# Fetching the values of even batches in two parts, and one chain of finishing steps for all twenty heads

## The chip, the cores and the metric

The kernel runs on one core of one Trainium2 chip. The metric is the device time of one execution in microseconds. The median of three runs of the kernel before is 429.22 us (427.91 to 430.65). The core has five engines that run side by side and wait for each other by semaphores: PE (TensorE), DVE (VectorE), ACT (ScalarE), POOL (GpSimd) and SP (SyncE, which here only issues transfers).

## The reference

Attention of 112 queries over 371 text tokens and 4 prompt tokens, for 8 batches and 20 heads of 16 channels, all in float32. The text probabilities are used a second time: the weighted mean of the context (512 wide) is normalised, and its inner products with the normalised prompts are added to the prompt scores.

```python
text_ehs = encoder_hidden_states[:, :-NUM_TOKENS]
ip_ehs = encoder_hidden_states[:, -NUM_TOKENS:]
...
probs_t = jax.nn.softmax(scores_t, axis=-1)
text_out = jnp.einsum('bhst,bhtd->bhsd', probs_t, v_t)
...
attn_scores = jnp.einsum('bhsd,bhnd->bhsn', q, k_ip) * attn_scale
qsem = jnp.einsum('bhst,bte->bhse', probs_t, text_ehs)
qsem = _l2norm(qsem)
ip_n = _l2norm(ip_ehs)
sem = jnp.einsum('bhse,bne->bhsn', qsem, ip_n)
fused = attn_scores + SEM_SCALE * sem
probs_ip = jax.nn.softmax(fused, axis=-1)
probs_ip = probs_ip * spatial_mask[None, None, :, None]
ip_out = jnp.einsum('bhsn,bhnd->bhsd', probs_ip, v_ip)
...
out = text_out + IP_SCALE * ip_out
out = out @ W_out + b_out
out = out + residual
```

## The kernel before

The twenty heads are worked on in five groups of four (`groups`), one step per batch and group; `b` is the batch, `g` the group, `a` the head within it. The kernel never forms the weighted context. It uses the matrix of inner products of the context rows with each other (the Gram matrix, `gram`, in the tile `ug`), so that the squared norm for a head is the probabilities times that matrix times the probabilities. The matrix is symmetric, so only its upper part is kept, with half weight on the diagonal blocks.

For each head the right operand of the products is a row of blocks in the tile `u`: the inner products of a block of 32 tokens with the tokens from there on, then the four prompts, a column of ones, and the 16 value channels of the head. One product round `j` (there are twelve, `BLK`) multiplies 32 transposed probability rows with such a block for the four heads of the group, each head in its own row band of the array and its own bank (`product`, L711 to L724). The bank then holds, for one head, the probabilities times the matrix (371 columns, read by `reduced` or `shared` to make the squared norm `ss`), and 21 further columns (the prompt products, the sum of probabilities, the values' sum), copied by ACT to `pvs` (`value_sums`).

How `u` is filled for a batch:

- The inner products: `gram_to_groups(b, (q,))` (L484) issues four transfers from `ug` to `u` for quarter `q` of the blocks, one for each row band. All four quarters are needed.
- The values: `values` makes them on PE in three chunks of 128 tokens (`vext`); `values_to_dram` (L561) writes them to DRAM (`vd`), `values_to_groups` (L581) fetches them back in the order of the row bands (`vr`), and before each group `placed` (L629) copies the group's 16 channels, chunk by chunk, from `vr` into `u` on POOL. Chunk `c` serves the product rounds 4c to 4c+3.

The probabilities take a similar way: `scores` on PE, `probabilities` (maximum on DVE, exponential on ACT, then a transfer `xg<-p` from SP), and `transposed` on DVE turns `xg` into `xgT`. Scores are made two groups ahead (`LEAD`).

The order of instructions on every engine is the order of the program text. Two steps are interleaved by `pair`, what has to be made for the next batches stands in `behind` (L1219), and pieces of work are generators that are advanced by `f`, `k`, `v`, `gr`, `q` and `run`. `turn` lists from which of three pools (`qd` four banks, `sc` two, `mm` two) the next banks of the array's output come. In an odd batch, `moved` (L1204) transfers the quarters 0, 1 and 3 behind the groups 0, 1 and 2, `behind` does quarter 2 at group 1, and the last chunk of values goes to DRAM at group 3 with the fetch of all values behind it (L1311 to L1320):

```python
            values_to_dram(nb, nc.sync, 2)
            tr(0)
            k(nb)
            f(b - 1, 2)
            tr(1)
            values_to_groups(nb)
```

`finish` turns `ss` and `pvs` of a batch into its output: a root and a reciprocal for the norm, a softmax over four prompts per head, the weighted prompt values, the division by the sum of probabilities, the output projection and the residual. ACT needs one table for the root and another for the exponential, loaded by `preload_act_table`.

The last batch (7) has no successor to interleave with, and its order is written out at the end (L1344 to L1427). There some heads' squared norms are made by ACT and POOL instead of DVE (`shared`: ACT copies the bank, POOL multiplies, ACT adds up). Batch 6 is finished within batch 7: `finish(b - 1, bd=...)` begins at group 1, takes its root at group 2, and its last projections stand behind the last product. Batch 7 itself is finished in two chains: `finish(b, (0, FULL * HC), ...)` for the first sixteen heads, begun before the last group's products, and `last_heads` for the last four; `projected_prompts` multiplies the last four heads' prompt values with the output matrix beforehand. The third key chunk of batch 7 is made by `last_keys` (L522) in two halves with two scores between.

Of the kernel before, what the change touches and what calls it, by code (L numbers as in the profile page):

```python
# [20 lines left out]
def kernel(  # L21
# [500 lines left out]
    def last_keys(b, ps):  # L522

        s = st[b]
        for e in range(NE):
            if e == NE // 2:
                yield
            nc.tensor.matmul(
                ps[:, :TT],
                wk_sb[:, e, FULL * P :],  # L530
                s["ctxT"][:, e, :TT],
                start=(e == 0),
                stop=(e == NE - 1),
            )
        nc.scalar.copy(s["kT"][:, FULL, :TT], ps[:, :TT])
        yield
# [44 lines left out]
    def values_to_groups(b):  # L581
        s = st[b]
        w = NG * D
        for a in range(GROUP):
            nc.sync.dma_start(
                s["vr"][a * RG : (a + 1) * RG].rearrange("p j g d -> p j (g d)"),
                s["vd"][:, a * w : (a + 1) * w].rearrange("(j i) x -> i j x", i=RG),
            )
# [86 lines left out]
    def probabilities(b, g, a):  # L675
# [13 lines left out]
        if (b, g, a) == (B - 1, NG - 1, 1):  # L689
            s["third"] = rows, p  # L690
            return
        nc.sync.dma_start(rows, p)
        if "third" in s:
            nc.scalar.dma_start(*s.pop("third"))
# [47 lines left out]
    def value_sums(b, g, a0=0):  # L742
        s = st[b]
        for h, ps in list(zip(groups[g], s["qd", g]))[a0:]:
            nc.scalar.copy(s["pvs"][:, h, :], ps[:S, TT:UW])  # L745

    def shared(b, g, n):
# [3 lines left out]
        if b == B - 1:  # L751
            t = work.tile([P, NE, TP], F32, tag="ctxT", name=f"shared_{b}_{g}")
            prods = [t[:S, a, :TT] for a, _ in some]
        else:

            t = work.tile([S, NIP, H, D], F32, tag="wv", name=f"shared_{b}_{g}", bufs=1)
            t = t.rearrange("p n h d -> p (n h d)")
            prods = [t[:, a * TP : a * TP + TT] for a, _ in some]
        p = s["p", g]
        for a, (h, ps) in some:  # L760
            if b == B - 1:
                nc.scalar.copy(s["pvs"][:, h, :], ps[:S, TT:UW])  # L762
# [32 lines left out]
    def finish(b, heads=(0, H), bd=None):  # L795
# [3 lines left out]
        h0, h1 = heads  # L799
        n = h1 - h0  # L800
        part = slice(h0, h1)

        def sm(name):
            return small.tile([S, H], F32, tag=name, name=f"{name}_{b}_{h0}", bufs=1)[:, :n]

        def sm4(name):
            return small.tile([S, H, NIP], F32, tag=name, name=f"{name}_{b}_{h0}", bufs=1)[:, :n]

        def over_ip(t):
            return t.unsqueeze(2).to_broadcast([S, n, NIP])  # L810

        pvs = s["pvs"][:, part]
# [8 lines left out]
        nc.vector.tensor_tensor(rn, s["ss"][:, part], z2, ALU.max)  # L821
        zr = sm("zr")
        attn = attn_ring[b % 2]
        ah = attn[:, :C].rearrange("p (h d) -> p h d", d=D)[:, part]

        def divided():
            eng.tensor_tensor(
                ah, pvs[:, :, NIP + 1 :], zr.unsqueeze(2).to_broadcast([S, n, D]), ALU.mult
# [17 lines left out]
        nc.vector.scalar_tensor_tensor(fu, fu, SEM_SCALE, s["ipl"][:, part], ALU.mult, ALU.add)  # L846
# [17 lines left out]
        i0, i1 = h0 * D // P, -(-h1 * D // P)  # L864
        if bd is not None:
            ps = bank(f"ps_wT_{b}")
            nc.tensor.transpose(
                ps[: n * NIP, :S], w.rearrange("s h n -> s (h n)"), ident[:S, :S]
            )
            wT = work.tile([P, NE, TP], F32, tag="ctxT", name=f"wT_{b}")[:, 0, :S]  # L870
            nc.scalar.copy(wT[: n * NIP], ps[: n * NIP, :S])
            yield

            ps = bank(f"ps_a_{b}_{h0}")
            for i in range(i0, i1):
                o = ps[:, i * S : (i + 1) * S]
                nc.tensor.matmul(  # L877
                    o, attn[:, i * P : (i + 1) * P], ident[:S, :S], start=True, stop=False
                )
                nc.tensor.matmul(  # L880
                    o,
                    bd[: n * NIP, i * P : (i + 1) * P],
                    wT[: n * NIP],
                    start=False,
                    stop=True,
                )
            yield

            aT = work.tile([P, NC, S], F32, tag="aT", name=f"aT_{b}_{h0}")
            nc.scalar.copy(  # L890
                aT[:, i0:i1], ps[:, i0 * S : i1 * S].rearrange("p (i s) -> p i s", s=S)
            )
            yield

            s["o"] = bank(f"ps_o_{b}", spare=True)
            for i in range(i0, i1):
                nc.tensor.matmul(  # L897
                    s["o"][:S, :C], aT[:, i, :], wo_sb[:, i, :], start=(i == 0), stop=(i == NC - 1)
                )
            if h1 < H:  # L900
                yield
                return
            yield
        else:
            yield from prompt_sums_and_projection(b, s, eng, part, n, h0, i0, i1, w, attn, ah)

        ob = work.tile([S, C], F32, tag="ob", name=f"ob_{b}", bufs=1)
        nc.vector.tensor_tensor(ob, s["o"][:S, :C], s["xb"], ALU.add)
# [6 lines left out]
    def prompt_sums_and_projection(b, s, eng, part, n, h0, i0, i1, w, attn, ah):  # L915
        wv = work.tile([S, NIP, H, D], F32, tag="wv", name=f"wv_{b}_{h0}", bufs=1)[:, :, :n]
        eng.tensor_tensor(
            wv,
            s["vip"][:, :, part],
            w.rearrange("p h n -> p n h").unsqueeze(3).to_broadcast([S, NIP, n, D]),  # L920
            ALU.mult,
        )
        eng.tensor_tensor(wv[:, :2], wv[:, :2], wv[:, 2:], ALU.add)
        eng.tensor_tensor(ah, ah, wv[:, 0], ALU.add)
# [546 lines left out]
```

## Time and profile before

| | |
|---|---|
| median of three runs | 429.22 us (427.91 to 430.65) |
| the profiled execution's own time | 432.04 us |
| its span, first to last instruction | 430.3 us |
| mean granted clock of PE | 0.995 |
| busy PE, DVE, ACT, POOL | 417.9, 330.5, 189.5, 111.6 us |
| transfers | 64.28 MB in 58063 packets, 18880 of them under 512 B |
| fetch of values, `vr<-vd` | 32 transfers of 120 KB |
| inner products, `u<-ug` | 128 transfers of 99 KB |
| probabilities, `xg<-p` | 159 transfers of 162.3 KB from SP, one from ACT |

Times in the profile are microseconds from the start of the span unless marked ns. A row of a timeline gives the start, the duration, the engine, the line and operation, the output and inputs, the count of merged instructions, and in brackets the engine's idle time before it and what ended it. SPq rows are the issuing of transfers, not their course. A row of a window table gives the window and its length, the busy time of PE, its weight loads, DVE, ACT and POOL with instruction counts, then the granted clock of PE, the busy share of the transfer engines and GB/s. Each float32 matmul shows as two instructions.

### The profile page before, as it was taken

What the parts mean: (1) busy time and instruction counts of PE and PEld (TensorE: products, weight loads), DVE (VectorE), ACT (ScalarE), POOL (GpSimd) and SP (SyncE); (2) the same over time, 40 slices, a digit from 0 to 9 for tenths busy, and PEclk for the clock granted to TensorE, in tenths of its full rate; (3) what the DMA queues carried; (4) which work ended last, traced back from release to release, by engine and by line L of the source; (5) the groups of instructions that cost most, each with busy time, mean ns of one, the idle gap of its engine ahead of it and who ended that gap; (6) DMA issues with size and microseconds to landing.
All of it is one profiled execution on the core that took longest, in us unless ns stands there. A gap on an engine that the chain in (4) does not pass through costs nothing. (4 is left out here: it accounts for less than half of the span.)

```text
span 430.3 us, 14013 instructions
## 1 busy us (share of the span) xinstructions
PE 417.9 (97%) x5515; PEld 325.6 (76%) x5515; DVE 330.5 (77%) x688; ACT 189.5 (44%) x646; POOL 111.6 (26%) x272
## 2 busy tenths in 40 slices
PE   8999999999999999999998999999997999999986
PEld 8766677797768887777677796879675887776783
DVE  4045877898888977877987887887988597778884
ACT  3253342336335642334542652515542364336793
POOL 4303110021332260031150351021060126026440
PEclk9999999999999999999999999999999899999999
DMA  7678967887553756767554746657655236663300
GB/s 246 166 195 240 199 167 184 177 185 171 134 144 104 173 146 158 175 138 177 133 157 122 174 123 159 164 135 170 169 138 144 79 102 168 162 161 107 97 2 28
DMA packets 58063, 64.28 MB, mean 149 GB/s; under 512 B 18880, under 2 KB 52024, under 8 KB 57998
## 3 DMA queue, kind: packets, MB, share of 16 engines
q1 hardware_dynamic: 57432, 62.67, 57.7%
q8 instruction: 44, 0.72, 0.7%
q10 hardware_dynamic: 566, 0.72, 0.5%
q14 instruction: 21, 0.17, 0.1%
HBM read 18.67 MB, written 5.32 MB: 56 GB/s over the span
## 5 line engine op out<-in xcount | busy, mean ns | idle before, releaser
L718 PE MATMUL ps_qd<-u,xgT 32*112 32x232 f32 (+11 forms) x3840 | 218.0, 354 | 4.9 <-POOL u L633 4.9
L718 PEld LDWEIGHTS ps_qd<-u,xgT 32*112 32x112 f32 x3840 | 186.2, 173 | 36.3 <-issue 8.4
L706 DVE STREAM_TRANSPOSE xgT<-xg 128x768 f32<-128x768 f32 (+1 forms) x63 | 122.2, 1970 | 3.9 <-DMA xg<-p 3.8
L683 ACT ACTIVATE p<-ps_s,nmx 112x371 f32<-112x371 f32 x160 | 85.6, 584 | 54.5 <-DVE nmx L679 42.6
L778 DVE CUSTOM_DVE_ANT_0 junk<-ps_qd,p 112x371 f32<-112x371 f32 x148 | 80.2, 542 | 34.8 <-ACT pvs L745 11.4
L679 DVE TENSOR_REDUCE nmx<-ps_s 112x1 f32<-112x371 f32 x160 | 77.2, 535 | 28.4 <-PE ps_s L666 27.0
L633 POOL COPY u<-vr 128x64 f32<-128x64 f32 x120 | 26.5, 236 | 200.6 <-PE ps_qd L718 113.1
L546 PE MATMUL ps_v<-wv_sb,ctxT 128*128 128x384 f32 (+1 forms) x192 | 63.8, 479 | 0.3 <-ACT kT L519 0.3
L666 PE MATMUL ps_s<-kT,qm 32*112 32x375 f32 (+1 forms) x320 | 61.0, 486 | 0.7 <-ACT shared L763 0.7
L546 PEld LDWEIGHTS ps_v<-wv_sb,ctxT 128*128 128x128 f32 x192 | 35.3, 190 | 21.2 <-ACT kT L519 1.2
L745 ACT COPY pvs<-ps_qd 112x21 f32<-112x21 f32 x150 | 21.3, 199 | 65.6 <-DVE ss L778 64.3
L512 PE MATMUL ps_k<-ctxT,wk_sb 128*128 128x371 f32 x136 | 45.8, 481 | 0.0
L512 PEld LDWEIGHTS ps_k<-ctxT,wk_sb 128*128 128x128 f32 x136 | 24.6, 190 | 13.4 <-ACT ctxT L424 0.5
L474 PE MATMUL ps_g<-ctxT 128*32 128x119 f32 (+11 forms) x672 | 33.3, 344 | 0.6 <-POOL ctxT L390 0.6
L666 PEld LDWEIGHTS ps_s<-kT,qm 32*112 32x112 f32 x320 | 28.4, 171 | 5.3 <-ACT shared L763 1.3
L474 PEld LDWEIGHTS ps_g<-ctxT 128*32 128x32 f32 x672 | 25.9, 110 | 8.1 <-issue 4.1
L553 ACT COPY vext<-ps_v 128x384 f32<-128x384 f32 (+1 forms) x24 | 11.2, 465 | 37.1 <-PE ps_v L546 37.0
L685 ACT COPY ipl<-ps_s 112x4 f32<-112x4 f32 x140 | 24.1, 172 | 0.0
L519 ACT COPY kT<-ps_k 128x371 f32<-128x371 f32 x17 | 8.0, 469 | 30.7 <-PE ps_k L512 30.7
L460 ACT ACTIVATE ug<-ps_g 128x375 f32<-128x375 f32 (+2 forms) x24 | 9.0, 377 | 27.9 <-PE ps_g L474 22.4
L353 DVE TENSOR_SCALAR qm<-ps_q,emask 128x224 f32<-128x224 f32 (+1 forms) x25 | 8.9, 396 | 15.4 <-PE ps_q L344 15.4
L402 DVE STREAM_TRANSPOSE ctxT<-ct 128x512 f32<-128x512 f32 x18 | 19.1, 1067 | 0.0
(161 smaller groups left out, 318.7 us busy)
## 6 DMA issues: line engine op xcount, KB each, us to landing
xg<-p SPq DMA_DIRECT2D x159, 162.3 KB
u<-ug SPq DMA_DIRECT2D x128, 99.0 KB
ct<-in_ctx_dram SPq DMA_DIRECT2D x24, 176.0 KB
vr<-vd SPq DMA_DIRECT2D x32, 120.0 KB
vip<-vipd SPq DMA_DIRECT2D x6, 560.0 KB
vd<-vext SPq DMA_DIRECT2D x14, 160.0 KB
vd<-vext SPq DMA_DIRECT2D x28, 40.0 KB
out_dram<-ob SPq DMA_DIRECT2D x8, 140.0 KB
```

Source lines behind the costliest of these rows:

```text
L474: nc.tensor.matmul(ps[p * RG : (p + 1) * RG, s0 : T - t0], ctxT[:, e, t0 + q * RG : t0 + (q + 1) * RG], ctxT[:, e, t0 + s0 : T], start=(e ...
L512: nc.tensor.matmul(ps[:, :TT], wk_sb[:, e, i * P : (i + 1) * P], s["ctxT"][:, e, :TT], start=(e == 0), stop=(e == NE - 1),)
L546: nc.tensor.matmul(ps[:, :w], ctxT[:, e, c * P : (c + 1) * P], wv_sb[:, e, :w], start=(e == 0), stop=(e == NE - 1),)
L633: nc.gpsimd.tensor_copy(region(b, c)[:, :, UV - c * P :], s["vr"][:, c * QN : (c + 1) * QN, g, :])
L666: nc.tensor.matmul(ps[:S, :w], qm[a * RG : (a + 1) * RG, i, r, j * S : (j + 1) * S], s["kT"][a * RG : (a + 1) * RG, i, :w], start=True, st ...
L679: nc.vector.tensor_reduce(nmx, ps[:S, :TT], AX.X, ALU.max, negate=True)
L683: nc.scalar.activation(p, ps[:S, :TT], AF.Exp, bias=nmx)
L685: nc.scalar.copy(s["ipl"][:, groups[g][a], :], ps[:S, TT:T])
L706: nc.vector.transpose(xT[:, j : j + n].rearrange("p j (k q) -> p q j k", q=QN), xg[:, :, j * RG : (j + n) * RG].rearrange("p q (j k) -> p ...
L718: nc.tensor.matmul(banks[a][:S, j * RG : UW], xT[a * RG : (a + 1) * RG, j, :S], region(b, c)[a * RG : (a + 1) * RG, p, q * RG :], start=(j ...
L745: nc.scalar.copy(s["pvs"][:, h, :], ps[:S, TT:UW])
L778: nc.vector.tensor_tensor_reduce(out=junk, in0=ps[:S, :TT], in1=s["p", g][:, a, :], scale=1.0, scalar=0.0, op0=ALU.mult, op1=ALU.add, accu ...
```

## The change

First, in the odd batches 1, 3 and 5 (which prepare the batches 2, 4 and 6), `values_to_groups` takes a range of chunks. Behind group 2 it fetches chunks 0 and 1, where the last quarter of inner products was transferred. At group 3 that quarter is transferred behind the last chunk's way to DRAM, and the fetch of chunk 2 follows it.

Second, the last batch. The finishing of batch 6 starts behind group 4 of batch 6 (root and table loads included) and its weights are made at group 1 of batch 7; all four heads of batch 6's last group go to `reduced` on DVE. `last_keys` runs in one piece in an `sc` bank. The scores of the last group come at rounds 1 and 2 of group 2, heads 0 and 1 first, and two of the four transfers of their probabilities are issued by ACT. The first chunk of `placed` for the last group is copied ahead of the products that POOL makes for group 2's heads. `finish` loses its range of heads, `last_heads` and `projected_prompts` go, and `ending` finishes all twenty heads of batch 7 in one chain behind the last product: it transposes the attention of sixteen heads, multiplies the prompt values of all heads with the output matrix (`ps_bw`), takes the root for all heads at once, and sums attention and prompts in one bank (`ps_o`).

```diff
-    def values_to_groups(b):
+    def values_to_groups(b, c0=0, c1=NT):
         s = st[b]
         w = NG * D
         for a in range(GROUP):
             nc.sync.dma_start(
-                s["vr"][a * RG : (a + 1) * RG].rearrange("p j g d -> p j (g d)"),
-                s["vd"][:, a * w : (a + 1) * w].rearrange("(j i) x -> i j x", i=RG),
+                s["vr"][a * RG : (a + 1) * RG, c0 * QN : c1 * QN].rearrange(
+                    "p j g d -> p j (g d)"
+                ),
+                s["vd"][c0 * P : c1 * P, a * w : (a + 1) * w].rearrange("(j i) x -> i j x", i=RG),
             )
...
             if g == 2:
-                gram_to_groups(nb, (3,))
+                values_to_groups(nb, 0, 2)
...
             tr(1)
-            values_to_groups(nb)
+            gram_to_groups(nb, (3,))
+            values_to_groups(nb, 2)
...
-        if (b, g, a) == (B - 1, NG - 1, 1):
-            s["third"] = rows, p
-            return
-        nc.sync.dma_start(rows, p)
-        if "third" in s:
-            nc.scalar.dma_start(*s.pop("third"))
+        eng = nc.scalar if (b, g) == (B - 1, NG - 1) and a % 2 else nc.sync
+        eng.dma_start(rows, p)
...
+        elif b % 2 == 0:
+            turn[:] = ["qd"] * 4 + ["mm"]
+            q(nb, 2)
+            f(b - 1)
+            k(nb)
+            nc.scalar.preload_act_table(AF.Sqrt)
+            tr(0)
+            f(b - 1, 2)
+            run(("f", b), lambda: finish(b, bd=bd[:, 0]), 2)
...
+    places = {
+        0: {0: (2, 3), 1: (0, 1)},
+        1: {0: (1, 2)},
+        2: {1: (0, 1), 2: (2, 3)},
+    }
     for g in range(NG):
         if g == 1:
-            keys3 = last_keys(b, ps_qd.tile([P, 512], F32, tag="qd", name=f"ps_k_{b}_{FULL}"))
-            next(keys3)
+            run(("f", b - 2), None)
+            last_keys(b, ps_sc.tile([P, 512], F32, tag="sc", name=f"ps_k_{b}_{FULL}"))
+            run(before, None, 2)
             coming(g, (3, 0))
-            next(keys3)
-            run(before, lambda: finish(b - 1, bd=bd[:, 0]))
+            run(before, None)
             own_channels(bd)
             with_bias(b)
...
+            if g == 3 and j == 3:
+                placed(b, g + 1, (0,))
+                next(sums)
+                transposed(b, g + 1)
+                drain(sums)
+            elif g < 3 and j == 2:
+                drain(sums)
+                transposed(b, g + 1)
...
+    drain(sums)
+    last = ending(b, bd[:, 1])
     next(last)
     run(before, None)
+    reduced(b, g, 0, 1)
+    value_sums(b, g, 1)
     next(last)
-    next(first)
+    value_sums(b, g, 0, 1)
+    reduced(b, g, 1)
     next(last)
-    next(first)
+    run(before, None)
+    for _ in range(3):
+        next(last)
+    run(before, None)
     next(last)
+    run(before, None)
+    drain(last)
     drain(gens[before])
```

The core of `ending`:

```python
        z2, rn = sm("z2"), sm("rn")
        eng.tensor_tensor(z2, z, z, ALU.mult)
        nc.vector.scalar_tensor_tensor(rn, z2, EPS * EPS, s["ss"], ALU.mult, ALU.max)
        nc.scalar.activation(rn, rn, AF.Sqrt)
        nc.scalar.preload_act_table(AF.Exp)
        divided(nc.vector, slice(h0, H))
        yield

        turned_attention(range(FULL, NC))
        ps_o = bank(f"ps_o_{b}", spare=True)
        for i in range(NC):
            nc.tensor.matmul(
                ps_o[:S, :C], aT[:, i, :], wo_sb[:, i, :], start=(i == 0), stop=False
            )
...
        ps = bank(f"ps_wT_{b}")
        nc.tensor.transpose(ps[:HN, :S], w.rearrange("s h n -> s (h n)"), ident[:S, :S])
        wT = work.tile([P, NE, TP], F32, tag="ctxT", name=f"wT_{b}")[:, 0, :S]
        nc.scalar.copy(wT[:HN], ps[:HN, :S])
        nc.tensor.matmul(ps_o[:S, :C], wT[:HN], bw, start=False, stop=True)
```

More of the change, by code (lines that the diff above doesn't have):

```diff
@@ L1405 @@
[L1405 to L1418 removed]
+        placed(b, g + 1, range(1 if g == 3 else 0, NT))
+        if g != 2:
+            next(sums)
+    drain(sums)
+    last = ending(b, bd[:, 1])
     next(last)
     run(before, None)
+    reduced(b, g, 0, 1)
```

331 lines of the change are left out of this document (131 added, 200 removed).

## The prediction

> **What bounds the kernel now.** I read the page's busy table first, then the waits of PE, the timeline around the longest of them, and the granted clock there.
>
> ```profile
> PE 417.9 (97%) x5515; PEld 325.6 (76%) x5515; DVE 330.5 (77%) x688; ACT 189.5 (44%) x646; POOL 111.6 (26%) x272
> ```
>
> PE is busy 417.9 of 430.3 us, and the diff takes only a few short matmuls from it. So an edit pays only where it closes one of PE's gaps (12.4 us in all) or shortens the chain behind the last product. The first line of the waits of PE (total, times, longest):
>
> ```profile
> PE ps_qd L718 <- POOL u L633: 4.9, 4, 2.4
> ```
>
> Products wait four times for GpSimd's copy of the values into `u` (`placed`, L633). Two of the four are where batch 3 gives way to 4 and batch 5 to 6; the timeline there, of SP and of PE, with the wait in brackets:
>
> ```profile
> 215.97 4.07 SPq L488 DMA_DIRECT2D u<-ug  x4
> 220.15 3.63 SPq L692 DMA_DIRECT2D xg<-p  x4
> 223.87 0.48 SPq L576 DMA_DIRECT2D vd<-vext  x1
> 226.29 1.87 SPq L585 DMA_DIRECT2D vr<-vd  x4
> ```
> ```profile
> 228.72 2.56 PE L718 MATMUL ps_qd<-u,xgT 32*112 32x296 f32 x56
> 232.37 2.02 PE L718 MATMUL ps_qd<-u,xgT 32*112 32x392 f32 x32 [1.08 <-POOL u L633]
> ```
> ```profile
> 323.64 0.49 SPq L576 DMA_DIRECT2D vd<-vext  x1
> 327.64 1.86 SPq L585 DMA_DIRECT2D vr<-vd  x4
> ```
> ```profile
> 328.31 2.83 PE L718 MATMUL ps_qd<-u,xgT 32*112 32x328 f32 x60
> 333.58 3.86 PE L718 MATMUL ps_qd<-u,xgT 32*112 32x392 f32 x33 [2.44 <-POOL u L633]
> ```
>
> The last values go to DRAM at 223.87 and 323.64. SP then stands idle until they have landed (1.94 and 3.51 us), and only then issues the fetch of all three chunks (`vr<-vd`). From the end of that issue to the first product it takes 4.21 us (228.16 to 232.37) and 4.08 us (329.50 to 333.58), the copy included. PE had been ready at 231.28 and 331.14, where its rows end. The longer stall has a second price, in the granted clock (the column behind the five busy times):
>
> ```profile
> 331.20:333.50 2.30, 0.00 (x0) 0.00 (x0) 1.67 (x2) 0.28 (x2) 0.21 (x2) 1.00 0.65 171
> 333.58:337.00 3.42, 3.42 (x33) 2.93 (x37) 1.32 (x5) 0.35 (x2) 0.44 (x3) 0.51 0.41 119
> ```
>
> For 3.42 us after the stall the clock is 0.51: another 3.42 x 0.49 = 1.7 us.
>
> [...]
>
> **Part A, the values of batches 2, 4 and 6.** The four fetches of 120 KB become four of two thirds, issued where the last quarter of inner products (`u<-ug`, four issues) stood, and four of one third in the old place; the four `u<-ug` move in between, right behind the last `vd<-vext`. SP gets four more issues in each odd batch, no other engine gets work.
>
> - The early fetch needs the first two chunks in DRAM. They are issued a whole round of `xg<-p` earlier (3.63 us at 220.15 for such a round), and 3.51 us is the longest landing shown above, so SP need not wait. `xg<-p` of the next group is queued behind; since the fetch takes 1.87 us to issue and `u<-ug` took 4.07, it goes out no later.
> - The late `u<-ug` fill SP's idle time in front of `vr<-vd`. [...]
> - The first copy needs the early fetch and all of `u<-ug`, not the last third. With 2.5 us of issue from 224.35 and 324.13 and 4.2 us to the product, PE can go on at 231.05 and 330.83, before it is ready (231.28, 331.14). With 4.07 it is 232.6 and 332.4, a stall of 1.3 us at both.
> - The last third is issued some 2 us later and needed by the ninth of a group's twelve rounds of products, 8/12 of 5.02 us (412.46 below) = 3.3 us on.
> - What is late next are the score banks, which ACT releases near 331; no quoted row separates them, so I charge 0.2 us.
>
> ```profile
> 252.92 2.49 SPq L488 DMA_DIRECT2D u<-ug  x4
> ```
>
> A takes 1.08 + 2.44 + 1.7 - 0.2 = 5.0 us from this execution. The ends: 5.2, and, with 1.3 us of stall at both places but the clock kept, 1.08 + 2.44 + 1.7 - 2.6 = 2.6; with the clock lost too, 0.9.
>
> **Part B, the last batch before its tail.** Three gaps, from the timeline of PE, then of POOL, DVE, SP and ACT:
>
> ```profile
> 391.42 1.51 PE L528 MATMUL ps_k<-ctxT,wk_sb 128*128 128x371 f32 x4 [0.55 <-ACT shared L763]
> 392.86 0.89 PE L666 MATMUL ps_s<-kT,qm 32*112 32x375 f32 x4
> 393.68 1.51 PE L528 MATMUL ps_k<-ctxT,wk_sb 128*128 128x371 f32 x4
> 395.12 0.60 PE L718 MATMUL ps_qd<-u,xgT 32*112 32x392 f32 x4
> ```
> ```profile
> 401.95 0.57 PE L666 MATMUL ps_s<-kT,qm 32*112 32x375 f32 x2 [0.68 <-ACT shared L763]
> ```
> ```profile
> 412.46 5.02 PE L718 MATMUL ps_qd<-u,xgT 32*112 32x392 f32 x96 [1.04 <-POOL u L633]
> ```
> ```profile
> 409.51 2.72 POOL L767 TENSOR_TENSOR shared<-shared,p 112x371 f32<-112x371 f32 x3 [2.30 <-ACT shared L763]
> 412.18 0.58 POOL L633 COPY u<-vr 128x64 f32<-128x64 f32 x3
> ```
> ```profile
> 409.93 3.00 DVE L706 STREAM_TRANSPOSE xgT<-xg 128x768 f32<-128x768 f32 x2 [0.59 <-DMA xg<-p]
> ```
> ```profile
> 394.95 11.69 SPq L692 DMA_DIRECT2D xg<-p  x7
> ```
>
> 1. `last_keys` moves from a "qd" bank that ACT is still emptying to an "sc" bank read long before, and its halves stay together: 0.55 us goes, and 0.1 to 0.2 for the missing interruption; 0.7.
> 2. The scores of the last group come one and two rounds later and begin with heads 0 and 1, whose banks ACT empties first: 0.68 becomes nothing, or 0.3 if ACT is late.
> 3. The first copy for the last group moves ahead of POOL's three products (2.72 us): 1.04 goes. Late next is DVE's first transpose, which waited for `xg<-p` (409.93, 3.3 us after the last issue ended at 406.64). Two of those four issues go to ACT's queue beside SP's, and the scores behind them come 1.3 us earlier, so the transpose should be done about when PE is. I take 0.8.
>
> Sum 2.2. Against it: two inner products of batch 6 go from ACT and POOL to DVE (542 ns each by the page), and its small operations move between the scores of groups 2 and 3, where GpSimd is at work. POOL there, DVE there, and DVE elsewhere:
>
> ```profile
> 394.25 2.09 POOL L619 TENSOR_SCALAR_AFFINE_SELECT bd<-bd 80x640 f32<-80x640 f32 x2
> ```
> ```profile
> 394.69 0.59 DVE L819 SCALAR_TENSOR_TENSOR z<-pvs 112x20 f32<-112x20 f32 x1
> 395.38 0.95 DVE L821 TENSOR_TENSOR rn<-ss,z 112x20 f32<-112x20 f32 x1
> ```
> ```profile
> 344.88 0.20 DVE L819 SCALAR_TENSOR_TENSOR z<-pvs 112x20 f32<-112x20 f32 x1
> 345.11 0.35 DVE L821 TENSOR_TENSOR rn<-ss,z 112x20 f32<-112x20 f32 x1
> ```
> ```profile
> L778 DVE CUSTOM_DVE_ANT_0 junk<-ps_qd,p 112x371 f32<-112x371 f32 x148 | 80.2, 542 | 34.8 <-ACT pvs L745 11.4
> ```
>
> The same two operations take 0.55 us elsewhere and 1.54 beside the two selections. Eight of batch 6's will stand beside GpSimd's products and selections. Two or three held up by some 0.5 us make DVE about 1 us late ahead of group 2's transpose, which has about that to spare: I charge 0.2, so this part gives 2.0, between 0.5 (no slack) and 2.4. The two table loads of batch 6 that move ahead of group 2's exponentials are 2 x 1.28 us (421.84 below) on an ACT that is 44% busy and hands to transposes a group later: nothing, and at most what is in the 0.5.
>
> [...]
>
> **The tail** runs from 417.48 (last product) to the sum at 426.89:
>
> ```profile
> 421.84 1.28 ACT L1001 ACT_TABLE_LOAD   x1
> ```
> ```profile
> 422.64 2.86 PE L897 MATMUL ps_o<-wo_sb,aT 128*112 128x320 f32 x10
> ```
> ```profile
> 426.89 0.49 DVE L1035 TENSOR_TENSOR ob<-ps_o,bd 112x320 f32<-112x320 f32 x1 [1.94 <-PE ps_o L1031]
> ```
> ```profile
> 427.41 0.33 SPq L1036 DMA_DIRECT2D out_dram<-ob  x1
> ```
>
> Before, DVE handled sixteen heads between the last four sums. Now the sums follow at once (4 x 0.54 and the norm, 2.5 us); the root waits behind ACT's copies for batch 6 (to about 3.2), then root and table (1.5), five steps to the weights (some 1.3): 6.0. But in front of the weights' transpose PE still has six output products of 0.57 (2.86 for five), the third only after ACT's last copy near 5.0: they end near 7.6. Transpose, copy and last product add about 1.4, so 9.0 against 426.89 - 417.48 = 9.41. Batch 6's output is now issued behind the last one, 0.33 us. I take zero, between 0.8 gained and 0.8 lost.
>
> **Sum, against the profiled execution:** its own time is 432.04 (span 430.3): 432.04 - 5.0 - 2.0 - 0 = 425.0. The median of the runs, 429.22, is 2.8 us below it, so the median run may not have paid for the slow clock. Without that the gain is 5.3, with it 7.0; I take 6.1 and get 429.22 - 6.1 = **423.1**, own range 421 to 425.5. One per cent, 4.3 us, is about what a measurement of this kernel tells from no change.
>
> **Rivals.**
> 1. The wait only changes its name: `u<-ug` lands little earlier than the values did. For: 4.07 us of issue is shown. Against: 2.49 too, and nothing in front of it waits for `vd`. A gives 0.9, B 2.0: 426.3.
> 2. DVE eats B: six operations held up by 0.5 us make it 3 us late, 1 us at each of two group starts. For: 0.95 at 395.38. Against: DVE's waits for scores between. A 4.4, B 0.2, tail -0.8: 425.4.
> 3. The other side: the late quarter of `u`, 396 KB behind a round of `xg<-p` and the early fetch's many small pieces, stalls all three boundaries (131 too) as 331 was stalled, clock included: 3 x 4.15 = 12.4 instead of 5.2, less B's 2.0: 429.22 + 5.2 = 434.4. It decides once PE goes on later than 233.7 and 333.6, 2.4 us after it is ready, that is, 6.8 us after the issue ends; 4.21 is the longest shown.
>
> **How the numbers follow.** Forecast 0.58, rivals 0.16, 0.15 and 0.11. Faster by over 1% (below 424.9): nine tenths of the forecast and two fifths of the second rival, 0.58. Slower by over 1% (above 433.5): most of the third, 0.10. Within: 0.32. The range takes in the first two rivals and the ends of A and B: 420.6 to 428.2.
>
> **What would show it.** Right: no wait of PE for `u` near 231 and 331, the clock 1.0 there, the first copy ahead of the third by some 2 us; from the end of group 0 (390.87) to the start of group 1 (395.12) of batch 7 about 3.5 us instead of 4.25; no wait at group 4. Wrong: POOL released by `u<-ug` while PE waits for it (rivals 1, 3); DVE's small operations near 0.9 us and PE waiting for transposes in batch 7 (2); more than 10.2 us from the last product to the last sum.

## The result, and the profile after

The changed kernel takes 426.6 us (median of ten runs, 425.5 to 427.53), the kernel before beside it 430.6 us (ten runs, 427.71 to 439.24). The ratio is 0.9903, with a 95% interval of 0.9874 to 0.9932: 4.2 us or 1.0% less. The profiled execution took 426.6 us, its span is 424.9 us.

The busy times of the page after, and the waits of PE (total, times, longest), without those that are as before:

```profile
PE 416.1 (98%) x5513; PEld 324.7 (76%) x5513; DVE 329.0 (77%) x681; ACT 185.9 (44%) x635; POOL 110.6 (26%) x271
...
PE ps_qd L713 <- POOL u L632: 1.3, 2, 0.9
PE ps_a L948 <- DVE attn L933: 0.7, 1, 0.7
PE ps_qd L713 <- DVE xgT L701: 0.4, 1, 0.4
PE ps_o L1015 <- ACT wT L1014: 0.4, 1, 0.4
```

PE's wait for `u` fell from 4.9 us in four places to 1.3 in two. These two are neither at the boundaries to batches 4 and 6 nor at the last group: one of 0.36 us is in batch 1, one of 0.89 us in front of batch 7. At the boundary to batch 6 the timelines of SP and POOL now read, with the granted clock there (the column behind the five busy times) below:

```profile
315.72 3.22 SPq L582 DMA_DIRECT2D vr<-vd  x4
319.74 3.58 SPq L689 DMA_DIRECT2D xg<-p  x4
323.42 0.49 SPq L573 DMA_DIRECT2D vd<-vext  x1
323.96 2.49 SPq L488 DMA_DIRECT2D u<-ug  x4
327.84 1.84 SPq L582 DMA_DIRECT2D vr<-vd  x4
...
329.48 0.42 POOL L632 COPY u<-vr 128x64 f32<-128x64 f32 x2 [6.22 <-DMA vr<-vd]
331.27 0.24 POOL L632 COPY u<-vr 128x64 f32<-128x64 f32 x1 [1.38 <-DMA vr<-vd]
```
```profile
331.20:333.50 2.30, 2.30 (x57) 1.92 (x55) 2.30 (x3) 0.55 (x3) 0.44 (x2) 1.00 0.32 83
333.58:337.00 3.42, 3.42 (x74) 3.08 (x69) 2.88 (x11) 1.52 (x7) 0.48 (x2) 1.00 0.63 182
```

The first copy starts about 1.8 us ahead of the third, PE is busy throughout both windows, and the clock stays at 1.00. In batch 7, the first products of the batch, `last_keys`, the first products of group 1 and those of the last group:

```profile
382.35 1.22 PE L713 MATMUL ps_qd<-u,xgT 32*112 32x392 f32 x10 [0.89 <-POOL u L632]
...
387.78 2.76 PE L526 MATMUL ps_k<-ctxT,wk_sb 128*128 128x371 f32 x8
...
390.49 0.58 PE L713 MATMUL ps_qd<-u,xgT 32*112 32x392 f32 x2
...
407.27 5.04 PE L713 MATMUL ps_qd<-u,xgT 32*112 32x392 f32 x96 [0.41 <-DVE xgT L701]
```

The end, of PE, DVE and SP:

```profile
417.71 1.78 PE L896 MATMUL ps_o<-wo_sb,aT 128*112 128x320 f32 x6
419.32 0.26 PE L1012 MATMUL ps_wT<-ident,w 112*80 112x112 f32 x1
...
420.81 0.49 DVE L1019 TENSOR_TENSOR ob<-ps_o,bd 112x320 f32<-112x320 f32 x1 [0.79 <-PE ps_o L1015]
...
421.33 0.35 SPq L1020 DMA_DIRECT2D out_dram<-ob  x1
421.73 0.41 SPq L905 DMA_DIRECT2D out_dram<-ob  x1
```

To see where time goes, I cut the traces at first products: of batch 5's last group, of batch 6's group 1 (the boundary lies between these two), of batch 7, and of its last group. The second trace of before, and the parts alone, belong to the experiments below.

| us from cut to cut | before | before, second trace | part A | part B | after |
|---|---|---|---|---|---|
| start to batch 5's last group | 326.05 | 325.78 | 325.93 | 326.80 | 326.67 |
| to batch 6's group 1 | 22.55 | 19.14 | 18.16 | 19.09 | 18.32 |
| to batch 7 | 36.77 | 36.69 | 36.63 | 36.96 | 37.36 |
| to its last group | 27.09 | 27.09 | 27.07 | 24.90 | 24.92 |
| to the end of the span | 17.84 | 18.00 | 21.01 | 17.55 | 17.63 |
| span | 430.3 | 426.7 | 428.8 | 425.3 | 424.9 |

The two traces of one and the same kernel before differ by 3.6 us, nearly all of it at the boundary to batch 6.

### The profile page after: what moved, and what is told of

The parts are those of the page before. It is cut to its first block, busy times and chain, and to the rows that moved or that the text cites. A ratio compares the mean times of both kernels' runs of the same rounds, so it can differ in the third digit from the quotient of the medians.

```text
span 424.9 us, 14020 instructions
## 1 busy us (share of the span) xinstructions
PE 416.1 (98%) x5513; PEld 324.7 (76%) x5513; DVE 329.0 (77%) x681; ACT 185.9 (44%) x635; POOL 110.6 (26%) x271
## 4 chain that ended last, share of the span: by engine, by line
PE 95%; DMA 1%; DVE 1%; ACT 1%; issue 0%; ACTq 0%; POOL 0%; SPq 0%; DVEq 0%; POOLq 0%
PE ps_qd L713 43%; PE ps_v L543 15%; PE ps_k L512 10%; PE ps_g L474 8%; PE ps_s L665 6%; PE ps_q L344 4%; PE ps_o L896 2%; PE ps_g L444 1%; DMA xg<-p 1%; PE ps_c L414 1%; PE ps_w L431 1%; PE ps_kv L280 1%; PE ps_k L526 1%; PE ps_k L503 1%; PE ps_x L336 0%
## 5 line engine op out<-in xcount | busy, mean ns | idle before, releaser
L766 DVE CUSTOM_DVE_ANT_0 junk<-ps_qd,p 112x371 f32<-112x371 f32 x150 | 81.2, 542 | 31.8 <-ACT pvs L740 10.9
```

The source lines that it names most:

```text
L766: nc.vector.tensor_tensor_reduce(out=junk, in0=ps[:S, :TT], in1=s["p", g][:, a, :], scale=1.0, scalar=0.0, op0=ALU.mult, op1=ALU.add, accu ...
```

## The experiments

**The kernel before, once more** (`before_again`, no edit).

> The kernel before, unchanged, for a second trace of it. Theory: the stall in front of batch 6's first products (2.44 us at 331.14) is there again, because nothing but the order of the transfers makes it, and so is the one in front of batch 4 (1.08 us). Open is the clock: if a stall of that length always costs it, the 3.4 us behind it run at about 0.5 again; if that was chance, the clock is 1.00 there and the span is some 1.7 us below 430.3. The second question is the start. After the change batch 1's first groups began 0.65 us later (70.15 against 69.50) and the step behind them lost another 1.66 us (102.39 against 100.08), in code that the change leaves alone: if this is scatter of the start, this trace may lie anywhere between the two; if the change caused it, it shows 69.5 and 100.1 again.

It took 428.38 us, span 426.7. The timeline of SP and of PE at the boundary to batch 6:

```profile
322.68 0.48 SPq L576 DMA_DIRECT2D vd<-vext  x1
326.49 2.10 SPq L585 DMA_DIRECT2D vr<-vd  x4
...
331.54 3.52 PE L718 MATMUL ps_qd<-u,xgT 32*112 32x392 f32 x56 [0.67 <-POOL u L633]
```

The stall is 0.67 us instead of 2.44, there is none in front of batch 4, and the clock is 1.00. From the end of the fetch's issue to the product it took 331.54 - 328.59 = 2.95 us, where the first trace took 4.08. To the first copy on POOL it took 3.92 and 3.79 us in the first trace (in front of batches 4 and 6) and 2.63 and 2.66 in this one. So the time that the fetch needs to land scatters by more than a microsecond, and the first trace had drawn a long one twice. The start scatters too: from group 0 of batch 1 to its group 2 this trace takes 21.88 us (88.94 to 110.82), the first one 20.13 (89.27 to 109.40), after 21.80 (89.91 to 111.71). So a kernel without the change shows that loss too. In the later traces of kernels with both parts the first line of the table lies between 325.3 and 331.4 us, a wider scatter than anything that the change gains.

**The two parts alone** (`part_a`, `part_b`). Part A is the kernel before with the ranges of chunks in `values_to_groups` and

```diff
-                gram_to_groups(nb, (3,))
+                values_to_groups(nb, 0, 2)
...
-            values_to_groups(nb)
+            gram_to_groups(nb, (3,))
+            values_to_groups(nb, 2)
```

and part B the changed kernel with these lines put back.

> Part A alone: the values of batches 2, 4 and 6 fetched in two parts with the late quarter between them, the last batch and its end as before. Theory (the two parts of the change add): the waits in front of batches 4 and 6 go, 1.08 + 2.44 us and 0 to 1.7 us of clock, so 3.5 to 5.2 us less than the kernel before, about 0.990, and the stretch from batch 7's first product to the end stays as before (385.37 to 426.89 = 41.5 us). Rival (the gain comes from the last batch): under 1.5 us, 0.997 or more.

> Part B alone: the new order of the last batch and the new end, the values fetched as before. Theory: both stalls are there again (about 1.1 and 2.4 us, with or without the clock), batch 7 from its first product to the last group's first product takes 24.9 us instead of 27.1, and the end is as long as before within 0.3 us; 2 us less than the kernel before, about 0.995. Rival (the whole gain is part B): 4 us, 0.990. Rival (DVE eats B): within 0.5 us, 0.999 or more.

Part A: 429.29 us beside 429.66, ratio 0.9974 (0.9944 to 1.0004). Part B: 427.99 us, 0.9929 (0.9893 to 0.9965). For A the number of the rival came, since 1 lies within its interval; B came out between its theory's 0.995 and its rival's 0.990, with the 24.9 us of the theory. The product, 0.9903, is the ratio of the whole change. With intervals this wide the exact agreement is luck; the numbers are in line with parts that add, of which B carries about three quarters. Among the runs with a mean clock of 0.997 or more the medians are 428.87 us for the kernel before (17 runs of 23), 428.04 for A (7 of 12) and 425.89 for B (6 of 12), so A's 0.8 us and B's 3.0 hardly come from a lost clock. By the table, A saves 19.14 - 18.16 = 1.0 us at the boundary against the second trace of before, B 2.2 us in batch 7 and 0.3 to 0.5 at the end. Part A's trace also shows what else its runs can lose: the old end, which this kernel keeps, lost the clock for 6.82 us (window, length, busy times, clock):

```profile
415.80:422.62 6.82, 6.82 (x17) 4.11 (x16) 2.77 (x16) 2.72 (x7) 0.00 (x0) 0.50 0.01 2
```

That is its 21.0 us from the last group on instead of 18.0. PE had waited there for 1.02 us at 407.79 and 0.53 at 414.17. The same end kept the clock in both traces of before. It does not explain A's median, for three of its runs with a mean clock of 1.000 took 429.2 to 429.3 us.

Counted over all traces, the old end lost the clock in two of four (`part_a`, `fetch_twice`) while PE still had products to make. In the ten traces with the new end, in either order of its products, it fell only after PE's last product (in the trace after at 422.35 us, 1.58 us behind it), or not at all. These are few, but they fit a gain of the new end of up to 3 us in some runs, which the table's traces of before do not show.

**Quarter and split, one at a time** (`quarter_only`, `split_only`). The changed kernel, first without the early fetch, then with the quarter back in its early place:

```diff
-                values_to_groups(nb, 0, 2)
...
-            values_to_groups(nb, 2)
+            values_to_groups(nb)
```
```diff
+                gram_to_groups(nb, (3,))
                 values_to_groups(nb, 0, 2)
...
-            gram_to_groups(nb, (3,))
             values_to_groups(nb, 2)
```

> The changed kernel with the quarter of inner products late, behind the last chunk's way to DRAM, and the whole fetch of the values behind it: the quarter moves, the fetch is in one piece. Theory (the fetch of the values is what counts): the four issues of u<-ug fit into the 2 to 4 us that SP waits there anyway, the whole fetch goes out when it did before, and PE waits for u in front of batch 6 as in part B alone (0.6 us, between 0.3 and 2.4) and hardly in front of batch 4. Rival (the moved quarter frees the queue, so that the last chunk reaches DRAM sooner): no wait at either place.

> The changed kernel with the last quarter of inner products back in its early place, ahead of the fetch of the first two chunks; only the fetch of the third chunk is late. Theory (the values' way through DRAM is what PE waited for, and fetching two thirds early is what removes it): no wait for u in front of batches 4 and 6, as in the changed kernel, and the first copy starts several us before PE's products instead of right ahead of them, since it no longer waits for a late u<-ug. Rival (the quarter had to make room): the probabilities' transfers behind the early fetch are issued 2 to 3 us later than in the changed kernel (221.00 and 319.74 there), and PE waits for DVE's transposes in groups 3 and 4 of the odd batches, 0.5 us or more at each.

My theory lost in `quarter_only`; in `split_only` it held, but the rival's cost came as well. With the quarter alone (425.75 us, span 424.0) PE waits for `u` at no boundary to an even batch. SP and POOL there:

```profile
322.68 0.36 SPq L573 DMA_DIRECT2D vd<-vext  x1
323.10 2.48 SPq L488 DMA_DIRECT2D u<-ug  x4
325.87 1.90 SPq L582 DMA_DIRECT2D vr<-vd  x4
...
330.56 0.59 POOL L632 COPY u<-vr 128x64 f32<-128x64 f32 x3 [7.50 <-DMA vr<-vd]
```

Counted from the first product of batch 5's last group (326.49), the last chunk leaves for DRAM at -3.81 us here, at -2.41 in the first trace of before (323.64, 326.05), -3.10 in the second, -3.00 in part B and -3.25 after. The quarter (3 to 4 us of issue) and a round of `xg<-p` stood ahead of it on SP, and with the quarter gone the whole fetch is early enough: its issue starts 0.62 us ahead of that product, in the second trace of before 0.71 us behind it. Of these 1.3 us the earlier start of the last chunk gives 0.7; where the rest comes from is not shown. The margin is small: the first copy starts 4.07 us after that first product (after the change 2.81, in the two traces of before 7.24 and 5.47), and in both traces of before PE was ready 5.09 us after it. The landing of the fetch alone scatters by as much as this margin (2.63 to 3.92 us from the end of its issue to the first copy in the two traces of before). With the split alone (428.2 us, span 426.5) PE does not wait for `u` there either, as the theory had it, but the cost that the rival named comes:

```profile
328.93 1.57 DVE L701 STREAM_TRANSPOSE xgT<-xg 128x768 f32<-128x768 f32 x1 [2.34 <-DMA xg<-p]
```
```profile
331.63 4.31 PE L713 MATMUL ps_qd<-u,xgT 32*112 32x392 f32 x55 [0.61 <-issue]
```

The first two chunks are in `u` at 324.95, but the early fetch now stands between the quarter and `xg<-p` (322.80 instead of 319.74). DVE waits 2.34 us for the probabilities, its maxima follow late, PE waits 0.61 us, and from cut to cut it takes 20.41 us (325.93 to 346.34) instead of 18.32. At the boundary to batch 4 there is no such wait, so the rival's "at each" did not come. After the change the same two copies start only at 329.48, 2.81 us behind the cut instead of 1.39 us ahead of it: there they wait for the late quarter, not for the early fetch, which was issued four microseconds earlier than here (315.72 against 319.79). The row of POOL names the fetch; the same row at the boundary to batch 4 (229.26 us, a wait of 4.53) names `u<-ug`.

**A stall made longer** (`fetch_twice`): the kernel before with `values_to_groups(nb)` issued twice.

> The kernel before with the fetch of all values of batches 2, 4 and 6 issued twice in a row, the same data to the same place, so that the first copy into u waits for the second fetch. It measures what a stall of PE at a batch boundary costs, and whether the granted clock falls behind it. The fetch takes 1.86 to 2.1 us to issue, so the copies come about 1.9 us later: in front of batch 6 a stall of 0.6 + 1.9 = 2.5 us (with the 2.44 of the first trace, 4.3), in front of batch 4 of 1 to 3 us (the two traces of before show 1.08 and none), in front of batch 2 of 0 to 2 us. Theory one (every stall of over about 1.4 us costs the clock for 3.4 us, another 1.7 us): the mean granted clock of nearly every run is 0.992 or less, the trace shows 0.5 behind each long stall, and the kernel is 3 x 1.9 + 2 x 1.7 = about 8 us slower, 1.019. Theory two (the clock falls only where the stall meets a window that the chip sets, so in some runs and at some places): the mean clock scatters between 1.00 and 0.985 from run to run, the trace shows 0.5 behind one or two stalls or none, and the time is 5 to 7 us longer, 1.012 to 1.016. Theory three (the first trace's clock had another cause): clock of 0.997 or more in all runs, and 1.008 to 1.013.

446.86 us (440.88 to 448.88), ratio 1.035 (1.030 to 1.041), twice what I expected, and a mean clock of 0.973 to 0.985 in all six runs. The three stalls, and the clock behind them:

```profile
140.45 3.52 PE L718 MATMUL ps_qd<-u,xgT 32*112 32x392 f32 x56 [1.74 <-POOL u L633]
242.06 5.21 PE L718 MATMUL ps_qd<-u,xgT 32*112 32x392 f32 x56 [2.64 <-POOL u L633]
346.48 6.21 PE L718 MATMUL ps_qd<-u,xgT 32*112 32x392 f32 x56 [3.88 <-POOL u L633]
```
```profile
140.45:144.00 3.55, 3.55 (x60) 3.51 (x64) 2.04 (x7) 0.53 (x3) 0.66 (x4) 1.00 0.65 181
242.80:246.20 3.40, 3.40 (x34) 3.34 (x32) 2.21 (x8) 0.71 (x4) 0.00 (x0) 0.51 0.48 127
345.70:352.50 6.80, 6.02 (x57) 5.16 (x61) 2.21 (x8) 0.71 (x4) 0.73 (x4) 0.53 0.42 119
```

A stall of 1.74 us cost no clock, 2.64 us cost 3.4 us at half, and 3.88 us cost 6.8 us, which began while PE still stood. So no theory fits whole, and the 1.4 us of theory one is shown by no run. That every run has a low mean clock is theory one's sign, that a stall of 1.74 us keeps the clock speaks for theory two, and the price is above both: in this trace the clock came back only after 3.4 or 6.8 us. The trace shows 0.5 in two more places: 99.50 to 102.90, in batch 1, behind a wait of 1.01 us, and 434.02 to 440.84, at the old end. So the 17 us are not the price of the three stalls alone. From cut to cut the three boundaries take 20.64, 23.22 and 25.07 us instead of 18.64, 18.59 and 19.14 in the second trace of before, which is 12.6 us; batch 1 up to group 2 takes 2.3 us more, the end about 3, the start up to batch 1 2.7. Whether the second fetch has a part in these is not shown.

**The early copy for the last group** (`copy_behind`): the changed kernel with

```diff
-                placed(b, g + 1, (0,))
                 next(sums)
+                placed(b, g + 1, (0,))
```

> The changed kernel with one swap: POOL makes the products of group 2's heads before it copies the first chunk of values for the last group, not behind. Theory (that copy was the whole of the old wait): in front of the last group's products PE waits for u again, 0.8 to 1.1 us instead of 0.41 us for the transpose, so the last group starts 0.4 to 0.7 us later. Rival (the transpose, which waits for the probabilities' transfer, is as late as the copy would be): 0.4 us as before, and only its name changes.

```profile
397.99 1.73 PE L713 MATMUL ps_qd<-u,xgT 32*112 32x392 f32 x15 [0.99 <-DVE xgT L701]
...
409.85 5.02 PE L713 MATMUL ps_qd<-u,xgT 32*112 32x392 f32 x96 [1.04 <-POOL u L632]
```

It took 429.15 us. The wait of before, 1.04 us, is back: theory right, worth 0.63 us. The other line was not expected: in front of group 2 PE waits 0.99 us for DVE. Batch 6's softmax is why; its operations with two inputs, in this kernel and then after:

```profile
390.66 0.98 DVE L830 TENSOR_TENSOR fu<-pvs,rn 112x80 f32<-112x80 f32 x1
391.68 0.77 DVE L831 SCALAR_TENSOR_TENSOR fu<-fu,ipl 112x80 f32<-112x80 f32 x1
...
392.75 0.76 DVE L834 TENSOR_TENSOR fu<-fu,mx 112x80 f32<-112x80 f32 x1
```
```profile
389.37 0.24 DVE L830 TENSOR_TENSOR fu<-pvs,rn 112x80 f32<-112x80 f32 x1
389.64 0.89 DVE L831 SCALAR_TENSOR_TENSOR fu<-fu,ipl 112x80 f32<-112x80 f32 x1
...
390.84 0.50 DVE L834 TENSOR_TENSOR fu<-fu,mx 112x80 f32<-112x80 f32 x1
```

**A better end** (`tail`, `tail_again`). The changed kernel with batch 6's output products right behind `ps_bw` and its output ahead of batch 7's:

```diff
     next(last)
     run(before, None)
-    for _ in range(3):
-        next(last)
-    run(before, None)
+    next(last)
+    run(before, None)
+    next(last)
+    next(last)
     next(last)
     run(before, None)
-    drain(last)
     drain(gens[before])
+    drain(last)
```

> The changed kernel with another order at the end: batch 6's six output products stand right behind the prompts' products (ps_bw), ahead of the last transpose and batch 7's own output products, and batch 6's output is issued before batch 7's. Theory: in the trace after the change PE waits 0.75 us for the attention of the last four heads, and later the weights' transpose, ready at 418.19, stands behind batch 6's products until 419.32. The products (1.78 us) fill that gap of 0.75 us, the weights' transpose starts near 418.7, the last sum near 420.1 instead of 420.81, and with the last transfer being the last output, issued right behind the last sum instead of 0.4 us later, the span is 0.6 to 1.2 us shorter, 0.997 to 0.9985 of the changed kernel. Rival (the end is set by the softmax chain on DVE and ACT, which the six products do not touch): last sum still near 420.8, gain 0 to 0.4 us.

> The changed kernel with batch 6's output products and output ahead, again, beside the changed kernel itself. Theory: in the traces the last sum comes 7.64 us after the last group's last product instead of 8.50, and the last transfer right behind it instead of 0.4 us later, so 1.2 us less than the changed kernel in the same call, 0.997 of it, and the clock kept in nearly every run. Rival (the 424.37 us against 426.6 were mostly the start of the runs): 0 to 0.6 us.

```profile
414.49 1.87 PE L896 MATMUL ps_o<-wo_sb,aT 128*112 128x320 f32 x6
...
418.05 0.27 PE L1012 MATMUL ps_wT<-ident,w 112*80 112x112 f32 x1
```

424.37 us (422.93 to 425.9) and 424.28 us (423.02 to 427.4), 0.985 of the kernel before both times (0.980 to 0.990 and 0.979 to 0.991). The weights' transpose starts 0.14 us behind its input instead of 1.1. From the last group's first product to the end it takes 16.1 and 16.2 us instead of 17.6, which is 1.5 us, more than expected: 0.9 of it up to the last sum (7.64 us behind the last product instead of 8.50), 0.6 behind it, where batch 6's output no longer stands. The changed kernel on the same chip as the second of them (`after_again`) took 426.17 us (423.96 to 431.19):

> The changed kernel, unchanged, timed beside its own variants of this call. Theory (the change takes both the typical time and the runs at a lower clock): 0.990 of the kernel before, between 0.986 and 0.994, and a mean granted clock of 0.997 or more in nearly every run, where about a quarter of the runs of before lie at 0.995 or less. Rival (that all ten of its first runs kept the clock was luck): some of the runs at 0.995 or less again, and a spread as wide as that of before.

Its ratio was 0.985 (0.978 to 0.992), but two of its six runs had a mean clock of 0.994. In its trace the clock fell in batch 1, behind a stall of 1.75 us in a place that the change does not touch. So keeping the clock in all ten first runs was partly luck. Over all runs of the experiments, 15 of 46 of the kernel before had a mean clock of 0.995 or less, 4 of 12 of part A and 5 of 12 of part B.

**Quarter alone with the better end, and a later softmax** (`quarter_tail`, `late_softmax`). The second moves batch 6's `run(before, ...)` from group 1 of batch 7 behind group 2's sums and behind the last transposes.

> The kernel with the changed tail, and of part A only the late quarter: the whole fetch of the values behind it, in one piece. Theory (what lay in front of the last chunk on SP's queue made the values late, and the moved quarter alone clears it): as fast as the kernel with both, within 0.5 us, and no wait for u in front of batches 2, 4 and 6. Rival (the fetch has to be split, and the one look at the quarter alone was a lucky start): waits of 0.3 to 2.4 us in front of batch 6 in the trace, a clock of 0.995 or less in some runs, and 0.5 to 2 us more time than with both.

> The kernel with the changed tail, with batch 6's softmax over its prompts (eight small operations of DVE, one exponential) behind group 2's products of batch 7 and its weights behind the last transpose, instead of between the scores of groups 2 and 3, where GpSimd multiplies and selects. It tests how DVE can eat part B: in two of six traces with the new last batch four of these operations took 0.5 to 1 us instead of 0.24 to 0.30, and PE waited 0.93 and 0.99 us for group 2's transposes; in the other four two of them were held up and PE did not wait. Theory: the operations take 0.2 to 0.3 us each in the new place, PE never waits for group 2's transposes, and the time is the changed tail's within 0.3 us in its undisturbed runs, some 0.3 us better in the median (a third of runs saving 0.95). Rival (the operations now delay the last group's transposes or sums): the wait of 0.41 us in front of the last group grows to 1 us or more.

The quarter alone took 425.55 us (423.79 to 429.36), 1.3 us above `tail_again`, with overlapping runs. Its trace has no wait for `u` at all, and 0.99 us for DVE in front of group 2; the first copy for batch 6 starts 4.44 us after the cut. Its profiled execution is its slowest run, 429.36 us; in it PE waited 2.23 us in batch 1, and the clock fell there (99.3 to 102.7). So in both traces without the split PE did not wait at a boundary; whether the split is worth its margin when the fetch lands late stays open. With the late softmax (424.69 us) PE does not wait in front of group 2, and the stretch from batch 7 to its last group takes 24.58 us, against 24.90 in `tail` and 25.76 in `tail_again`, where that wait was 0.97. But the end takes 16.6 us, and no difference is left in the time.

## Why the prediction was right, and where it was not

Predicted were 423.1 us within 420.6 to 428.2; it is 426.6. Of a gain forecast as 6.1 us, 4.0 to 4.2 were measured; the kernel before measured 1.4 us higher than the median that the forecast started from. Against the profiled execution the steps gave 425.0, and it took 426.6. That rival 1 named 426.3 is chance, for its mechanism did not come.

- **Part A's mechanism, as it was written, happened.** The four late `u<-ug` took 2.49 us to issue (2.5 was taken; of the 4.07 us at 215.97 in the first trace of before one issue took 2.16 us and the other three 0.58 to 0.59, and what held the one up is not shown), the probabilities behind the early fetch went out no later (the fetch took 3.22 us to issue, not the 1.87 that I had taken, but still less than the 4.07 of the quarter), PE's waits went, and the first copy led by 1.8 us (about 2 was named). Against the first trace it gains 22.55 - 18.32 = 4.2 us at the boundary to batch 6 and 1.4 at the one to batch 4 (226.19 to 246.17 before, 228.15 to 246.74 after), less 0.6 for a longer wait in front of batch 7 (0.89 instead of 0.30): 5.0. That this is the predicted sum is chance, for that wait lies between none and 0.89 us in the traces with both parts and no step named it. What is shown is that the two stalls and the slow clock were gone, 5.6 us against this one execution.
- **The step that failed is the size of A for the runs, because its durations came from one execution.** I saw that the median lay 2.8 us below that execution and doubted only the slow clock, so I kept 5.3 to 7.0 as the gain. The stalls themselves, 2.44 and 1.08, were as unusual: 0.67 and none in the second trace of before, 0.62 and none in part B. A typical A is 0.8 to 1.0 us at the boundary to batch 6. The lower end of 0.9 that I gave stood for another mechanism, late quarters with a lost clock, so that it is near is chance. With 0.9, B's 2.2 and 0.2 of the tail the change is worth 3.3 us; 4.0 to 4.2 were measured. Where the rest comes from is not shown. Long stalls in other runs of before can make it up, and so can the old end's lost clock, seen in two of four traces; the tail's step, which I put at nothing, had no term for that.
- **A's reason was half right.** I took the split for what removes the wait and the quarter for what has to make room. In two traces moving the quarter was enough, and in one the split alone cost. The score banks, for which I charged 0.2 us as late next, fit the 0.61 us of PE in that run; the row names no releaser, so that is argued.
- **Part B:** 27.09 - 24.92 = 2.17 us against 2.0, and the same in part B alone. Its pieces fell otherwise than priced. From `last_keys` to group 1 it took 2.7 us (387.78 to 390.49), not 3.5: with the halves together, the scores and the first products overlap. From there to the last group it gained 17.34 - 16.78 = 0.56 us instead of 1.5, since these scores now stand in it, and 0.41 us of wait for the transpose remained, the next limit that I had named.
- **The tail:** the last sum 8.50 us behind the last product (412.31 to 420.81) for the 9.0 predicted and 9.41 before, and 0.68 us lost behind it where 0.33 were charged. Net 0.2 us gained, predicted nothing, against a trace of before that kept the clock at its end.
- **The 1.6 us by which the profiled execution missed the sum** lie mostly in batch 1, where the first trace of before was quick (20.13 us against 21.80); a start later by 0.6 is nearly made up by 0.3 won back in batch 3 and by the gains of B and the tail beyond their steps. They belong to no step.
- **Rivals.** The first did not come: the copies no longer wait while PE does. The second, DVE eating B, is real but not the rule: in four of nine traces with B's new order (not counting the late softmax) PE waited 0.93 to 0.99 us in front of group 2, and in these four three operations took 0.76 to 1.02 us, where in the other five one took 0.89 or 0.90 and the rest 0.53 or less. With the late softmax three of them took 0.24 us each, and PE did not wait. In the prediction's price of this rival, 4.4 us for A stands in no sum; with the forecast's own gain it would have been 425.7 instead of 425.4. The six operations held up by 0.5 us that it counts are shown by no run: of batch 6's softmax no trace has more than three above 0.53 us, and operations with one input, like the reduction and the reciprocal between them, kept their 0.22 to 0.30 us in all nine. What held an operation up is not shown: the same line (L830) took 0.98 us in `copy_behind` and 0.24 us after the change, both times while POOL was at its three products (389.63 to 392.34 and 388.48 to 391.23 us). The third did not come, but `fetch_twice` shows its price: in its trace three stalls of 1.74, 2.64 and 3.88 us cost 12.6 us at the boundaries, clock included. The 12.4 that I had worked out were for three stalls of 2.44 us that all lose the clock once, so the sum is right and its parts fell otherwise.

## What to carry to other kernels

Before a stall is priced, take a second trace of the same kernel: a wait for a transfer's way through DRAM was 2.44 us in one execution and 0.67 in the next, while the waits for an engine's work came out alike (1.04 and 1.02 at the last group). When a transfer lands late, look at what stands ahead of its first leg on the issuing queue before cutting its last leg in two. At the end of a kernel, put other work's matmuls into the gaps ahead of the last chain, not between its links, and issue the other work's output first: that gave 0.9 and 0.6 us here. Before the parts of a change are added up, look at the clock of each run: the old end lost it in two of four traces, which cost about 3 us in these and nothing in the others.

## What the runs showed of the hardware

The granted clock fell to half for 3.4 us or twice that (3.42, 3.40, 6.80 and 6.82 us in four places), and the length of a stall alone does not say whether it falls: behind 2.44 and 2.64 us it fell, behind 1.74 us it did not, yet it fell behind 1.75 us in batch 1 of `after_again` and behind 1.01 us in batch 1 of `fetch_twice`. Read in steps of 0.1 us, the four falls of `fetch_twice` begin at 99.51, 242.87, 345.27 and 434.02 us. Their distances, 143.36, 102.40 and 88.75 us, are 42, 30 and 26 times 3.413 us. The two falls of the first trace of before, at 333.62 and 429.19 us, lie 95.57 us apart, 28 times 3.413. So within each of these two runs the falls lie whole steps of 3.413 us apart, though PE went on 1.65 us ahead of the first fall of `fetch_twice` (97.86), 0.81 ahead of the second (242.06) and 1.21 behind the third (346.48). In the 3.41 us ahead of the four falls PE was busy for 2.40, 0.81, 0.74 and 2.79 us; in the step of 3.41 us from 137.06, behind which no fall came, for 1.68. What calls for a fall is not shown, and the busy time of this profile does not decide it, since 1.68 us kept the clock and 2.40 and 2.79 us lost it. In the old end of part A, waits of only 0.53 us among short products stood in the 3.4 us ahead of the fall, and PE was busy for 2.87 of 3.40 us (412.40 to 415.80).
